# A four-layer graph network: slots for near edges alone in layer 0, a ranking of nodes for each layer, paced scatters and bulk loads

## The chip, the cores and the metric

The kernel runs on one core of a Trainium2 chip. The metric is the device time of one execution in microseconds (us), so lower is better. The core's engines are PE (matrix multiply; its weight loads are listed as PEld), DVE (vector), ACT (scalar, activation functions), POOL (general purpose) and SP (here only an issuer of DMAs). Each engine works through its own instructions strictly in order, so an instruction that waits holds up everything queued behind it on that engine. That holds for the DMAs that SP and POOL issue too.

## The reference

There are 128 graphs of 64 nodes with 128 features, `x[128,64,128]`, and one weighted adjacency `adj[128,64,64]` for all layers. Four layers follow each other, each as `x = layernorm(x + layer(x, adj))`. Layers 0 and 1 are convolutions with a filter that a small network makes from each edge's length; they are the costly ones.

```
layer 0:  f  = exp(coeff * (d - offset)^2)                 # 20 values per pair of nodes
          W  = ssp(f @ fw1 + fb1) @ fw2 + fb2              # 128 values per pair of nodes
          W *= 0.5 * (cos(d * pi / 5) + 1) * (d < 5)       # nothing is left from the cutoff 5 on
          agg[i] = sum_j y[j] * W[i,j],   y = x @ w_in2f
layer 1:  the same shape with 64 Gaussians; W *= adj twice, so only nonzero entries count
layers 2, 3: two graph convolutions with a normalised adjacency
```

In layer 0 an entry `adj = 0` is a distance of zero and not a missing edge: it has the full weight, and one and the same filter. Entries of 5 and more add nothing in layer 0, but they do count in layer 1. Counted from the reference's own inputs, a node has 15.88 nonzero entries on average, 13.22 of them below the cutoff.

## The kernel before, in words

Only nonzero entries go through the filter network. A first stage counts the nonzero entries of each node, ranks the 64 nodes of a graph by that count, and gives rank class `r` (eight nodes each) a fixed number of slots, `CAPS[r]`. Eight classes have 34+23+...+15 = 165 slots together, a graph has 8 x 165 = 1320 (`GSLOTS`). If some graph does not fit, a flag sends the whole job to `dense_stack` afterwards; this does not happen with these inputs.

Graphs are handled in 64 pairs (`NP`), and eight pairs form a set. For each set, `compact`

- scatters the adjacency rows into rank order in DRAM, with 8 indirect DMAs from POOL (one per pair, `perm`, line 807), and reads them back (`ad`, line 815);
- takes the largest entries of each row eight at a time on DVE: `max` (line 823), `max_index` (826), `match_replace` (830). `ROUNDS` says how often per class, 24 rounds in all;
- copies the values into `dc` (POOL, line 837) and the indices into `jc` (ACT), makes the cutoff weight `rc` with seven DVE instructions and one sine on ACT, and `a2` (the squares, for layer 1) on POOL, and stores all four to DRAM (lines 851, 852, 877, 878).

Set 0 is compacted ahead of the main loop. The other seven are interleaved with the first twenty pairs or so of it, by a queue called `early`, from which up to ten steps are taken per chunk.

The main loop takes layer 0's 64 pairs and then layer 1's. A pair is done in three chunks of 440 slots per graph. For a pair, `loads` brings `d`, `j` and the weight `w` from DRAM, each copied to many partitions (lines 907 to 918; buffers for two pairs). Per chunk there are:

- ACT: the Gaussians of the next pair (`gaussians`, the square and the exponential of `d`);
- DVE: `hot`, a weighted one-hot matrix that selects a neighbour for each slot (line 1276);
- PE: `px` (first filter layer, line 1291), `pw` (second, line 1304), `pg` (gathering the neighbours' features with `hot`, line 1316);
- ACT: `h` twice (softplus as exponential and logarithm) and `g` (a copy out of PSUM);
- DVE: `m = (pw + b2) * g` (line 1329), and after a pair's last chunk eight `agg` sums over slots (line 1345).

The chunks are software-pipelined: `message` works on the chunk from three iterations back, `filter_out` and `gather` on the one from two back. After four pairs (a quad) `node_after` does the output network, `zero_share` (the share of zero entries, read from `perm`), the way back from rank order (from `code_dram`), and a layernorm, whose power of -0.5 runs on POOL (line 1064). Layers 2 and 3 (`graph_convs`) run beside layer 1 for quads that are done.

The order on each engine is made at build time by the framework's scheduler from the order of the calls, its own estimates and the dependencies; it may hoist work. A DRAM tile is tracked as a whole: two scatters into one `perm` tile are ordered, and the second waits until the first has landed. Before the change the scheduler placed the scatters of sets 0 to 4 in turn (set 0, 1, 2, 3, 4, 0, 1, ...), so set 0's eighth scatter is the 36th of the program.

Of the kernel before, what the change touches and what calls it, by code (L numbers as in the profile page):

```python
# [11 lines left out]
F32 = mybir.dt.float32  # L12
# [6 lines left out]
P = 128  # L19
A = 64  # L20
# [18 lines left out]
CAPS = (34, 23, 21, 20, 19, 17, 16, 15)  # L39
ROUNDS = tuple(-(-k // 8) for k in CAPS)  # L40
BASES = tuple(sum(CAPS[:r]) for r in range(8))
SLOTS = sum(CAPS)
GSLOTS = 8 * SLOTS
CHUNK = GSLOTS // 3
# [530 lines left out]
def sparse_stack(ctx: ExitStack, tc: tile.TileContext, t: dict, out: bass.AP, flag):  # L575
# [26 lines left out]
    place = const.tile([NB, A], F32, name="place")  # L602
    odd = const.tile([P, 4 + NS], F32, name="odd")
    nc.gpsimd.memset(odd, 0.0)
    with (
# [4 lines left out]
        some = pre.tile([NB, A, A], BF16, name="some")  # L610
        for q in range(4):
            cut = slice(16 * q, 16 * (q + 1))
            nc.sync.dma_start(entries[:, cut, :], adj[:, cut, :])
            nc.vector.tensor_scalar(some[:, cut, :], entries[:, cut, :], 0.0, None, ALU.is_gt)

        def count(v, name):
# [11 lines left out]
        degree = count(some, "degree")  # L628


        tie = pre.tile([NB, A], I32, name="tie")
        nc.gpsimd.iota(tie, pattern=[[-1, A]], base=A - 1, channel_multiplier=0)
        key = pre.tile([NB, A], F32, name="key")
        nc.vector.tensor_copy(key, tie)
        nc.vector.scalar_tensor_tensor(key, degree, float(A), key, ALU.mult, ALU.add)
        before = pre.tile([NB, A, A], BF16, name="before")
        nc.vector.tensor_tensor(
            before, key.unsqueeze(1).to_broadcast([NB, A, A]),
            key.unsqueeze(2).to_broadcast([NB, A, A]), ALU.is_gt,
        )  # L640
        rank = count(before, "rank")

        r_i = pre.tile([NB, A], I32, name="r_i")
        nc.vector.tensor_copy(r_i, rank)
        p_i = pre.tile([NB, A], I32, name="p_i")
        nc.vector.tensor_scalar(p_i, r_i, 7, 3, ALU.bitwise_and, ALU.logical_shift_left)
        nc.vector.tensor_scalar(r_i, r_i, 3, None, ALU.logical_shift_right)
        nc.vector.tensor_tensor(p_i, p_i, r_i, ALU.bitwise_or)
        nc.vector.tensor_copy(place, p_i)


        caps = pre.tile([NB, 8], F32, name="caps")
        most = pre.tile([NB, 8], F32, name="most")
        for r in range(8):
            nc.gpsimd.memset(caps[:, r : r + 1], float(CAPS[r]))
            nc.gpsimd.memset(most[:, r : r + 1], 8.0 * r)
        over = pre.tile([NB, 8, A], F32, name="over")
        nc.vector.tensor_tensor(
            over, degree.unsqueeze(1).to_broadcast([NB, 8, A]),
            caps.unsqueeze(2).to_broadcast([NB, 8, A]), ALU.is_gt,  # L660
        )
        number = pre.tile([NB, 8], F32, name="number")
        nc.vector.tensor_reduce(number, over, AX.X, ALU.add)
        nc.vector.tensor_tensor(number, number, most, ALU.is_gt)
        nc.vector.tensor_reduce(odd[:, 0:1], number, AX.X, ALU.add)

        below = pre.tile([NB, A * A], F32, name="below")
        nc.scalar.activation(
            below, entries.rearrange("g i j -> g (i j)"), AF.Relu, scale=-1.0, accum_out=odd[:, 1:2]
# [3 lines left out]
        for i, (w, b, k) in enumerate(  # L673
# [13 lines left out]
            nc.vector.tensor_scalar(odd[:, 2 + i : 3 + i], b1, X_LIMIT, None, ALU.is_gt)  # L687
# [42 lines left out]
    row_i = const.tile([P, 3], I32, name="row_i")  # L730
    nc.gpsimd.iota(row_i, pattern=[[0, 3]], base=0, channel_multiplier=1)
    nc.vector.tensor_scalar(row_i[:, 1:2], row_i[:, 1:2], 15, 6, ALU.bitwise_and, ALU.logical_shift_left)
    nc.vector.tensor_scalar(row_i[:, 2:3], row_i[:, 2:3], 1, 6, ALU.bitwise_and, ALU.logical_shift_left)

    row = const.tile([P, 3], F32, name="row")
    nc.vector.tensor_copy(row, row_i)

    near_i = const.tile([P, 1], I32, name="near_i")
    nc.vector.tensor_scalar(near_i, row_i[:, 0:1], 63, None, ALU.bitwise_and)
    near = const.tile([P, 1], F32, name="near")  # L740
    nc.vector.tensor_copy(near, near_i)
# [3 lines left out]
    nc.vector.tensor_scalar(goes, place, row[:, 1:2], None, ALU.add)  # L745
    tp = ps_n.tile([P, 512], F32, tag="n", name="goes_t")
    nc.tensor.transpose(tp[0:A, 0:P], goes, ident)
    index = const.tile([P, NP], U32, name="index")
    by_pair = tp[0:A, 0:P].rearrange("i (p b) -> i p b", b=2)
    for b in range(2):  # L750
        nc.vector.tensor_copy(index[b * A : (b + 1) * A, :], by_pair[:, :, b])

    code = const.tile([P, A], BF16, name="code")
    nc.vector.tensor_scalar(code, place, row[:, 2:3], None, ALU.add)
    code_dram = dram.tile([NB, A], BF16, name="code_dram")
    nc.sync.dma_start(code_dram, code)

    a_all = const.tile([P, NP, A], F32, name="a_all")
    a_pairs = adj.rearrange("(p b) i j -> (b i) p j", b=2)
    x_all = const.tile([P, NP, C], F32, name="x_all")  # L760
    x_pairs = x.rearrange("(p b) n c -> (b n) p c", b=2)
    perm = [dram.tile([16 * A, A], F32, name=f"perm{s}") for s in range(NS)]
    slots = {
        name: [dram.tile([P, SLOTS], dt, name=f"{name}_dram{s}") for s in range(NS)]
        for name, dt in (("d", F32), ("j", BF16), ("rc", F32), ("a2", F32))
# [30 lines left out]
    def compact(sets):  # L796
# [5 lines left out]
        n = len(sets)  # L802
        dc = cpt.tile([P, n * SLOTS], F32, tag="dc", name=f"dc{sets[0]}")
        jc = cpt.tile([P, n * SLOTS], BF16, tag="jc", name=f"jc{sets[0]}")
        for i, s in enumerate(sets):
            for p in range(8 * s, 8 * (s + 1)):
                nc.gpsimd.indirect_dma_start(  # L807
                    out=perm[s][:, :],
                    out_offset=bass.IndirectOffsetOnAxis(ap=index[:, p : p + 1], axis=0),
                    in_=a_all[:, p, :],  # L810
                    in_offset=None,
                )
                yield
            ad = cpt.tile([P, 8, A], F32, tag="ad", name=f"ad{s}", bufs=2)
            nc.sync.dma_start(ad, perm[s].rearrange("(q r) j -> q r j", r=8))
            yield
            top = cpt.tile([P, 8, 40], F32, tag="top", name=f"top{s}", bufs=2)
            at = cpt.tile([P, 8, 40], U16, tag="at", name=f"at{s}", bufs=2)
            for k in range(max(ROUNDS)):
                now = [r for r in range(8) if ROUNDS[r] > k]  # L820
                cut = slice(8 * k, 8 * (k + 1))
                for r in now:
                    nc.vector.max(out=top[:, r, cut], in_=ad[:, r, :])
                    yield
                for r in now:
                    nc.vector.max_index(out=at[:, r, cut], in_max=top[:, r, cut], in_values=ad[:, r, :])  # L826
                    yield
# [617 lines left out]
```

## Time and profile before

| | us |
|---|---|
| median of 3 runs | 2127.33 |
| lowest, highest | 2122.57, 2143.56 |
| the profiled execution, whole | 2122.68 |
| its span in the profile | 2120.9 |
| first `px` matmul of pair 0 | 117.8 |
| first `hot` of layer 0, first `hot` of layer 1 | 122.0, 998.7 |
| busy: PE, DVE, ACT, POOL | 1775.3, 1692.6, 1489.6, 210.1 |

Span and whole execution differ by 1.8 us. The profile's times start with the first instruction. Where a stretch table is shown, its columns are: the stretch in us, its length, the busy time of PE, PEld, DVE, ACT and POOL with the number of instructions in brackets, the granted clock of PE as a share of full speed, the mean busy share of the 16 DMA engines, and GB/s. In a list in order of time, a line gives start and duration, engine, source line, operation and tiles, and in brackets the idle time of the engine before it with what ended that.

### The profile page before, as it was taken

What the parts mean: (1) busy time and instruction counts of PE and PEld (TensorE: products, weight loads), DVE (VectorE), ACT (ScalarE), POOL (GpSimd) and SP (SyncE); (2) the same over time, 40 slices, a digit from 0 to 9 for tenths busy, and PEclk for the clock granted to TensorE, in tenths of its full rate; (3) what the DMA queues carried; (4) which work ended last, traced back from release to release, by engine and by line L of the source; (5) the groups of instructions that cost most, each with busy time, mean ns of one, the idle gap of its engine ahead of it and who ended that gap; (6) DMA issues with size and microseconds to landing.
All of it is one profiled execution on the core that took longest, in us unless ns stands there. A gap on an engine that the chain in (4) does not pass through costs nothing.

```text
span 2120.9 us, 22583 instructions
## 1 busy us (share of the span) xinstructions
PE 1775.3 (84%) x6827; PEld 794.1 (37%) x6827; DVE 1692.6 (80%) x4476; ACT 1489.6 (70%) x1662; POOL 210.1 (10%) x296
## 2 busy tenths in 40 slices
PE   0087888899999999999988988888888898888874
PEld 0032333333333333333344444444444444444433
DVE  3395999988888888888778887887888888878863
ACT  0075778798888888888877766776677776777730
POOL 4714000000000000000000010010000101001010
PEclk9987989999999999999999999999999999999985
DMA  7154443444444444445544444534345344453300
GB/s 198 41 130 105 102 100 88 107 111 108 108 108 108 117 114 116 113 113 123 133 122 96 120 104 99 130 91 120 92 111 125 95 121 104 102 133 89 94 5 7
DMA packets 111392, 222.77 MB, mean 105 GB/s; under 512 B 35972, under 2 KB 61596, under 8 KB 111260
## 3 DMA queue, kind: packets, MB, share of 16 engines
q1 hardware_dynamic: 105040, 218.06, 41.9%
q0 software_dynamic: 2048, 2.10, 0.3%
q10 hardware_dynamic: 4172, 1.07, 0.3%
q8 instruction: 56, 0.92, 0.2%
q14 instruction: 76, 0.62, 0.1%
HBM read 212.49 MB, written 8.67 MB: 104 GB/s over the span
## 4 chain that ended last, share of the span: by engine, by line
PE 35%; DVE 32%; ACT 16%; issue 6%; DMA 5%; POOL 5%; SPq 0%; ACTq 0%; DVEq 0%; POOLq 0%
PE pw L1304 11%; DVE m L1329 7%; DVE agg L1345 7%; PE pg L1316 7%; PE px L1291 6%; ACT h L713 5%; ACT g L713 4%; DVE hot L1276 4%; ACT d L713 3%; DVE x_all L1067 2%; ACT na L713 2%; DMA d<-d_dram 2%; PE hw L1213 2%; POOL perm L807 2%; POOL rs L1064 2%
## 5 line engine op out<-in xcount | busy, mean ns | idle before, releaser
L713 ACT ACTIVATE g<-pg 128x880 f32<-128x880 f32 x384 | 344.4, 897 | 306.8 <-PE pg L1316 247.7
L1316 PE MATMUL pg<-hot,ys 64*128 64x440 f32 x1536 | 420.0, 599 | 37.2 <-ACT g L713 37.1
L1345 DVE TENSOR_REDUCE agg<-m 128x16 f32<-128x544 f32 (+7 forms) x1024 | 442.6, 487 | 0.0
L1304 PE MATMUL pw<-h,w_L_gnn_fw 128*128 128x440 f32 x768 | 354.9, 573 | 56.0 <-DVE m L1329 52.3
L713 ACT ACTIVATE h<-h,half 128x880 f32<-128x880 f32 (+1 forms) x385 | 394.6, 1025 | 8.3
L1304 PE MATMUL pw<-h,w_L_gnn_W2T 128*128 128x440 f32 x768 | 333.8, 557 | 3.1 <-DVE m L1329 3.1
L1329 DVE SCALAR_TENSOR_TENSOR m<-pw,c_L_gnn_fb,g 128x440 f32<-128x440 f32 x384 | 240.4, 667 | 62.7 <-ACT g L713 62.5
L1329 DVE SCALAR_TENSOR_TENSOR m<-pw,c_L_gnn_b,g 128x440 f32<-128x440 f32 x384 | 242.5, 667 | 57.5 <-ACT g L713 56.5
L1276 DVE SCALAR_TENSOR_TENSOR hot<-j,near,w 128x440 f32<-128x440 bf16 x384 | 249.9, 672 | 21.7 <-PE pg L1316 21.5
L713 ACT ACTIVATE h<-px,c_L_gnn_b 128x880 f32<-128x880 f32 x192 | 189.9, 989 | 77.2 <-PE px L1291 77.2
L1316 PEld LDWEIGHTS pg<-hot,ys 64*128 64x128 f32 x1536 | 124.3, 189 | 277.3 <-ACT h L713 86.1
L1064 POOL TENSOR_TENSOR rs<-rs,neg_half 128x4 f32<-128x4 f32 x64 | 64.5, 1008 | 1514.3 <-DVE rs L1063 1502.3
L1304 PEld LDWEIGHTS pw<-h,w_L_gnn_fw 128*128 128x128 f32 x768 | 130.4, 196 | 215.0 <-DVE m L1329 122.2
L1291 PE MATMUL px<-d,w1t 64*128 64x440 f32 x768 | 197.6, 563 | 4.4 <-ACT h L713 4.4
L1291 PE MATMUL px<-d,fw 32*128 32x440 f32 x768 | 198.8, 594 | 2.5 <-ACT d L713 1.5
L713 ACT ACTIVATE h<-px,c_L_gnn_fb 128x880 f32<-128x880 f32 x192 | 190.2, 991 | 8.8 <-PE px L1291 2.7
L1304 PEld LDWEIGHTS pw<-h,w_L_gnn_W2T 128*128 128x128 f32 x768 | 133.5, 194 | 150.3 <-issue 70.3
L713 ACT ACTIVATE d<-d,neg_off 96x880 f32<-96x880 f32 (+1 forms) x128 | 154.0, 1203 | 15.2 <-DMA d<-d_dram 14.2
L1291 PEld LDWEIGHTS px<-d,fw 32*128 32x128 f32 x768 | 59.1, 187 | 130.0 <-ACT h L713 64.8
L1291 PEld LDWEIGHTS px<-d,w1t 64*128 64x128 f32 x768 | 73.3, 190 | 71.2 <-issue 39.9
L713 ACT ACTIVATE jc<-at 128x16 bf16<-128x16 uint16 (+7 forms) x64 | 11.3, 215 | 109.4 <-DVE at L826 106.8
L713 ACT ACTIVATE d<-d 128x1320 f32<-128x1320 f32 x64 | 83.1, 1299 | 0.5
(182 smaller groups left out, 1754.6 us busy)
## 6 DMA issues: line engine op xcount, KB each, us to landing
j<-j_dram SPq DMA_DIRECT2D x256, 165.0 KB
w<-rc_dram SPq DMA_DIRECT2D x128, 330.0 KB
w<-a_dram SPq DMA_DIRECT2D x128, 330.0 KB
d<-d_dram SPq DMA_DIRECT2D x128, 330.0 KB
d<-d_dram SPq DMA_DIRECT2D x192, 110.0 KB
x_all<-in_x_dram SPq DMA_DIRECT2D x8, 512.0 KB
cb<-code_dram SPq DMA_DIRECT2D x32, 128.0 KB
out_dram<-gz SPq DMA_DIRECT2D x16, 256.0 KB
```

The lines of the kernel that those rows point to most:

```text
L713: last = nc.scalar.activation(out_, in_, func, **kw)
L807: nc.gpsimd.indirect_dma_start(out=perm[s][:, :], out_offset=bass.IndirectOffsetOnAxis(ap=index[:, p : p + 1], axis=0), in_=a_all[:, p, :] ...
L1064: nc.gpsimd.tensor_tensor(rstd, rstd, neg_half[:, 0:n], ALU.pow)
L1067: nc.vector.tensor_scalar(dst[:, s, :], y[:, s, :], mv[:, s, 0:1], rstd[:, s : s + 1], ALU.subtract, ALU.mult,)
L1213: nc.tensor.matmul(ps[:, s, :], lhsT=lhs(s), rhs=rhs(s), start=True, stop=True)
L1276: nc.vector.scalar_tensor_tensor(hots[n][:, at], j[:, at], near, wt[:, at], ALU.is_equal, ALU.mult)
L1291: nc.tensor.matmul(ps[:, b, 0:CHUNK], lhsT=w["w1"][rows, :], rhs=d[rows, col : col + CHUNK], start=True, stop=True,)
L1304: nc.tensor.matmul(ps[:, 0:CHUNK], lhsT=c["w"]["w2"], rhs=c["h"][:, b, :], start=True, stop=True)
L1316: nc.tensor.matmul(ps[:, b, 0:CHUNK], lhsT=y[rows, :], rhs=hots[c["n"]][rows, at], start=True, stop=True,)
L1329: nc.vector.scalar_tensor_tensor(messages[n][:, b, at], c["pw"][b][:, 0:CHUNK], c["w"]["b2"], c["g"][:, b, :], ALU.add, ALU.mult,)
L1345: nc.vector.tensor_reduce(av[:, :, r], v[:, :, BASES[r] : BASES[r] + CAPS[r]], AX.X, ALU.add)
```

## The change

The counting stage now also counts the entries below the cutoff, and ranks the nodes twice: `places[0]` by the number of nonzero entries below the cutoff, `places[1]` by the number of all nonzero entries. Each layer gets its own slots: layer 0 has 141 per class set (chunks of 376 slots), layer 1 has 162 (chunks of 432).

`compact` works in the order of `places[0]`. It turns the values around (zero becomes -1e30, the rest their negatives), so `max` now finds the nearest edges first. It takes 30 rounds instead of 24, because all edges of a row are kept for layer 1, up to 40. The first ones become layer 0's slots (`pack(0, s)`). A new step `spread(s)` scatters the sorted rows once more, into the order of `places[1]`, with 8 more indirect DMAs (`rows1`), reads them back and packs layer 1's slots (`pack(1, s)`). For set 0 it first repeats the 8 scatters of the adjacency with the extra column that carries the second rank (`perm_again`).

The bulk loads of `a_all` and `x_all` for sets 1 to 7 no longer stand ahead of the loop: `load_set(s+1)` is issued in the loop, after the loads of a pair. The scatters are held back by `mark(n)`, a one-column copy on POOL that reads pair `n`'s `hot`: a set's first scatters come after `hot` of its pair 1 (modulo 8), the second ones after that of pair 4. The cosine weight is made per set, with one sine for each of eight sets (before: five sines for all). Layer 1's weights and the constants of layers 2 and 3 are asked for later. `early` gives up to 8 steps per chunk instead of 10.

```diff
-CAPS = (34, 23, 21, 20, 19, 17, 16, 15)
+CAPS = ((30, 21, 18, 17, 16, 14, 13, 12), (33, 23, 21, 19, 18, 17, 16, 15))
+ROUNDS = (5, 4, 4, 4, 4, 3, 3, 3)
...
+            nc.vector.tensor_scalar(near[:, cut, :], entries[:, cut, :], CUTOFF, None, ALU.is_lt)
...
+        rank(0, close)
+        rank(1, degree)
+        crowded(0, close)
+        crowded(1, degree)
...
+    def mark(n):
+        return nc.gpsimd.tensor_copy(marks[:, n % 2 : n % 2 + 1], hots[n][:, 0:1])
+
+    def scatter(into, rows, at, behind):
+        with tc.issue_after(behind.ins) if behind is not None else nullcontext():
+            nc.gpsimd.indirect_dma_start(
+                out=into, out_offset=bass.IndirectOffsetOnAxis(ap=at, axis=0),
+                in_=rows, in_offset=None,
+            )
...
+    def compact(s, behind=None):
+        ad = cpt.tile([P, 8, A + 1], F32, tag="ad", name=f"ad{s}", bufs=2)
+        for p in range(8 * s, 8 * (s + 1)):
+            scatter(perm[s][:, :], a_all[:, p, 0 : A + (s > 0)], index[:, p : p + 1], behind)
+            yield
+        nc.sync.dma_start(ad[:, :, 0 : A + (s > 0)], perm[s].rearrange("(q r) j -> q r j", r=8))
...
+        nc.vector.tensor_scalar(zero, av, 0.0, FAR, ALU.is_equal, ALU.mult)
+        nc.vector.tensor_tensor(av, zero, av, ALU.subtract)
...
+        yield from pack(0, s, top, at)
+        tops[s] = ad, comb, at
+
+    def spread(s, behind):
+        ad, comb, at = tops.pop(s)
+        if s == 0:
+            for p in range(8):
+                scatter(perm_again[:, :], a_all[:, p, :], index[:, p : p + 1], behind)
+                yield
...
+        goes = cpt.tile([P, 8], U32, tag="goes", name=f"goes1_{s}")
+        nc.vector.tensor_scalar(goes, ad[:, :, A], row[:, 4:5], None, ALU.add)
+        nc.gpsimd.tensor_copy(comb[:, :, 1, :], at)
+        yield
+        for r in range(8):
+            scatter(
+                rows1[s].rearrange("q a k -> q (a k)"),
+                comb[:, r, :, :].rearrange("p a k -> p (a k)"), goes[:, r : r + 1], behind,
+            )
+            yield
+        rows = cpt.tile([P, 8, 2, 40], F32, tag="rows", name=f"rows_{s}")
+        nc.sync.dma_start(rows, rows1[s].rearrange("(q r) a k -> q r a k", r=8))
+        yield
+        yield from pack(1, s, rows[:, :, 0, :], rows[:, :, 1, :])
...
-    for s in range(1, NS):
-        nc.sync.dma_start(a_all[:, part(s), :], a_pairs[:, part(s), :])
-        nc.sync.dma_start(x_all[:, part(s), :], x_pairs[:, part(s), :])
...
+            if k == 0 and n < NP:
+                if n % 8 == 0 and n + 8 < NP:
+                    load_set(n // 8 + 1, slot_data[n + 1][3])
+                if n % 8 == 1 and n + 8 < NP:
+                    early.append(compact(n // 8 + 1, mark(n)))
+                if n % 8 == 4:
+                    early.append(spread(n // 8, mark(n)))
+                if n == NP // 2:
+                    layers.append(filter_layer(1))
+                if n == NP - 3:
+                    early.extend((settle(), late_constants()))
...
-        run(early, 10)
+        run(early, 8)
```

## The prediction

> **What bounds the kernel now.** I read the page first (busy shares, the strip of slices), then the table of stretches, then the list in order of time.
>
> ```profile
> PE 1775.3 (84%) x6827; PEld 794.1 (37%) x6827; DVE 1692.6 (80%) x4476; ACT 1489.6 (70%) x1662; POOL 210.1 (10%) x296
> ...
> PE   0087888899999999999988988888888898888874
> ...
> DVE  3395999988888888888778887887888888878863
> ```
>
> No single engine is full; the strips show three parts. In the first two slices (53 us each) PE does nothing: the head, until the first `hot` at 122.0. In slices 4 to 7 DVE reads 9 and PE 8. Then PE reads 9.
>
> ```profile
> 220.00:320.00 100.00, 82.72 (x289) 33.31 (x288) 96.31 (x423) 71.76 (x96) 6.20 (x24) 0.91 0.42 106
> 527.41:629.97 102.56, 97.99 (x374) 39.39 (x372) 84.24 (x184) 87.79 (x96) 2.02 (x2) 1.00 0.45 110
> ```
>
> While sets are compacted, DVE is busy 96% and sets the pace; afterwards, 51.2 us per four pairs, PE is busy 96% and DVE has 18% left. Layer 0 lasts from 122.0 to 998.7, 876.7 us. What an edit costs thus depends on whether it falls on a stretch with DVE work to spare.
>
> **Fewer slots.** PE has 12.25 us per pair (97.99 / 8). Per chunk the chain gives `pw` 1.67, `pg` 0.94, `px` 0.94, together 3.55; times 376/440 that is 3.03, so a pair of layer 0 needs 10.7. DVE has 10.53 per pair. The sums of 544 and 240 elements take 711 and 394 ns, 1.04 ns per element; 64 elements less in 6 `m` and 3 `hot` save 0.60 and 384 less in `agg` 0.40, leaving 9.5. Layer 1 goes from 440 to 432: about 70% of its 1046 us follows the slots, so 1.8% x 0.85 of that saves **12 us**.
>
> **Compaction.** Eight `MAX8` take 1.10 us, an index search 0.195, a replacement 0.19. 24, 24 and 16 of them cost 11.0 us per set; 30, 30 and 22 cost 14.1. Some fifteen other DVE rows of 0.1 to 0.6 us (turning values, ties, mask, weight) bring 4.2, the degrees 1.3: 19.6 per set. Before, this fell in the first 300 us; now it lies in layer 0 up to pair 55, beside DVE work. DVE then has 9.5 + 19.6/8 = 11.95 per pair, 95.6 per set, 99.5 at 96% busy. It, not PE, sets the pace there. Three pairs of each set have no ranking work in the built order and go by PE: 10.7 at a granted clock of 0.95 (between the 0.91 and 1.00 of the two stretches) is 11.2, against DVE's 10.1 with what is left of the set, so 3.5 more. That makes 103 us per set without any new wait, against 102.5 in the steady part before.
>
> **The scatters become a chain.** This is the change's largest unknown.
>
> ```profile
> 106.93 0.97 POOL L807 DMA_INDIRECT perm<-a_all,index  x1 [0.30 <-issue]
> 109.30 1.07 POOL L807 DMA_INDIRECT perm<-a_all,index  x1 [1.40 <-DMA perm<-a_all,index]
> ...
> 117.17 0.99 POOL L807 DMA_INDIRECT perm<-a_all,index  x1 [1.40 <-DMA perm<-a_all,index]
> ```
>
> Before, scatters of five (later three) sets took turns, 1.27 us apart, so that each had long landed when the next into the same tile came. In the built program of the new kernel a set's eight stand one behind the other, and each waits for the one before. What a landing takes, two rows tell. The scatter at 109.30 waited for the one issued at 104.27, 5.0 us earlier, with a pair's loads in the queues; the one at 117.17 for that of 111.95, 5.2. In the quiet,
>
> ```profile
> 72.17 0.96 POOL L807 DMA_INDIRECT perm<-a_all,index  x1 [0.30 <-issue]
> ...
> 74.33 0.32 SPq L815 DMA_DIRECT2D ad<-perm  x1
> ```
>
> set 0's eighth had landed 2.2 us after its issue. So a step of the chain (issue, landing, next issue) costs 2.3 to 5.2 us. The loop's DMA share is 0.45, and 2.3 + 0.45 x 2.8 gives **3.5**, my value.
>
> What waits for the chain: in DVE's order, the turning of values (line 889) stands 17.7 us of work behind the `hot` that releases the chain, 19 us at the pace above. The chain needs 0.6 + 8 x 3.5 + 0.4, and the read-back 3.5 (in the old loop 3.0 to 5.0), so 32.5: DVE stands still for **13.5 us**, and all of `hot`, `m`, `agg` queue behind it. The second chain has six scatters ahead of the copies into `dc` on POOL, which DVE's line 853 needs 15.6 us after the mark: 0.6 + 5 x 3.5 + 2.6 = 20.7, **5 us** more. Because DVE sets the pace there, nothing covers these stalls: `pw` can't run ahead further than its PSUM buffers, which `m` frees.
>
> Behind the waiting instructions stand other things. On SP the read-backs of both chains have the `d` loads of a pair two ahead behind them. `d` is wanted by ACT two chunks after DVE goes on, some 8 us, and such a load lands in about 6, so I add nothing; without that cover it would be up to 6 per set. On POOL the layernorm's power of every second quad stands behind the second chain, its read-back and eight copies, 42 us after the mark; its user on DVE comes after 41.5 us of work plus the 5 us stall, so it is hidden too, and is 3 late at steps of 5. POOL's own new work, 16 scatters, a mark, and some 20 copies of 0.2 us per set, is some 22 us of 120. 18.6 per set, seven sets: **130 us**. At steps of 2.3 us it is 4 per set, at 5.2 it is 41.
>
> [...]
>
> The scatter's own time on POOL is 0.97 us on average with DVE idle (45 to 74 us) and 0.97 beside `MAX8` and its kin (94 to 104), so I add nothing for DVE. [...] No copy of DVE lies beside a scatter in those rows, while the new scatters lie in the loop. [...]
>
> **The rest of layer 0.** Each set has its own sine; the two table loads of 1.28 on ACT are a bubble. ACT is near 10.7 per pair too; 0 to 20, I take 10. The two powers of 10.6 us on POOL, on the chain before at 165, move behind set 7's scatters and ahead of a layernorm's: 6. In sum: pairs 0 to 7 at PE's pace (8 x 10.7 at a clock of 0.93) 92, six sets 6 x 103 = 618, pairs 56 to 63 without compaction 8 x 11.0 = 88, stalls 130, 10 and 6: 944, **67 more** than 876.7.
>
> **The head.** Before `index`, the second count adds 3.8 us, the second comparison 4.4 and its count 3.1, small ones 3: the first scatter comes 14.3 us later, at 41.7. But set 0's eighth is now the eighth and not the 36th: eight steps of 2.4 end at 61, against 74.3. The read-back took 5.1 to the first `MAX8` (79.47), so rounds start near 67 and take 14. From the old rounds' end (101.2) to the first `hot` were 21 us, so `hot` comes near 103, 19 earlier. The old rounds contain 11 us (82 to 93) in which DVE waited for nothing that the profile shows; whether that returns is open, and scatter steps of 5 would take 21. Range 25 gained to 5 lost; I take **15 gained**. That the bulk loads (6 MB) leave the head is inside this: in the loop they add to a DMA share of 0.45 and cost at most what the step's upper bound holds.
>
> **The sum**, against the profiled execution: 2122.7 + 67 - 15 - 12 = **2163 us**, 1.7% above the median of 2127.33. 1% is about what a measurement can tell from no change.
>
> **Rivals.**
> - *The chain is short* (the other side, faster). Scatters land in the gaps between the loads, at 2.3 per step, and lines 889 and 853 find their data nearly there. Per set the stalls are 8 x step - 14.5 and 5 x step - 12.4, so it decides below 2.9 us per step: there they are 11 in all, and the total is 1% under the median. For it: 2.2 in the quiet, and a stall of DVE itself empties the queues. Against: the waits of 5.0 and 5.2. At 2.3: 130 falls to 28, 2163 - 102 = about 2060, with the full gain of the head 2050.
> - *The chain is loaded throughout*, because the bulk loads go into the loop just ahead of the first scatters: 5 us per step, 38 per set, 2163 + 136 = 2300. For it: the same two rows. Against: half of the time the DMA engines are idle.
> - *The slots do not suffice*, and the dense version runs as well. Counted from the reference's inputs, no graph exceeds the new classes; I give it nothing.
>
> **How the numbers follow.** Steps between 3 and 4 us, 2110 to 2215: 0.45, of which 0.17 is within 1%. Short chain: 0.32, faster. Loaded chain: 0.18. Other causes 0.05, split. So faster 0.34, the same 0.17, slower 0.49. The range takes in nearly all of the short chain and most of the loaded one: 2040 to 2280.
>
> **What would show it.** In the new profile: `px` and `pw` near 0.49 and 0.48 us each instead of 0.58 and 0.55; DVE idle before line 889, released by the read-back, about 13 us seven times; POOL's scatters 3.5 us apart with the DMA of the one before as releaser; the first `hot` near 105; layer 1 beginning near 1050. I am wrong if line 889 does not wait, if PE rather than DVE is full in pairs 8 to 55, or if DVE, PE and ACT, all at 10.7 to 12 us per pair, hold each other up more than 96% busy allows.

## The result, and the profile after

The changed kernel takes **2197.87 us** (median of 4 runs, 2184.42 to 2204.98) against 2134.48 us of the kernel before (median of 4, one of them measured beside the changed kernel). The ratio is 1.029, with a 95% interval of 1.021 to 1.038: slower by about 3%. The forecast was 2163, with a range of 2040 to 2280. Runs more than 1.5% above their kernel's fastest (one of experiment 1, two of experiment 5) are left out of the ratios below, but not out of the medians.

The profiled execution took 2202.33 us (span 2200.5), 79.7 more than the one of before. It splits as follows; "head" is the time to the first `hot` of layer 0, "layer 1" what follows the first `hot` of layer 1.

| | before | after | difference | forecast |
|---|---|---|---|---|
| head | 122.0 | 97.6 | -24.4 | -15 |
| layer 0 | 876.7 | 961.2 | +84.5 | +67 |
| layer 1 and the end | 1122.2 | 1141.7 | +19.5 | -12 |

From the page of the changed kernel, busy times and three strips (forty slices of 55 us, in tenths):

```profile
PE 1793.1 (81%) x6828; PEld 850.8 (39%) x6828; DVE 1679.1 (76%) x4824; ACT 1404.3 (64%) x1727; POOL 305.4 (14%) x482
...
PE   0378898887978886898989888898888998888874
...
DVE  5577787778787775886888887788878877778773
...
PEclk9978888898988887898999999999999999999985
```

DVE, which the prediction held to be full in layer 0, reads 7 and 8 there. PE has fewer slots to work through and yet is busy 18 us longer than before. The strip of the granted clock points to why: 8 through most of layer 0, where the kernel before has 9 from its seventh slice to the end of layer 0:

```profile
PEclk9987989999999999999999999999999999999985
```

The stretch table of the changed kernel; the columns are those explained with the profile of before (the number in tenths or hundredths behind POOL is the granted clock). The rows are pairs 16 to 23, 56 to 63, and, in layer 1, 32 to 39:

```profile
328.00:450.70 122.70, 102.21 (x374) 46.77 (x372) 95.94 (x337) 82.46 (x116) 22.77 (x40) 0.85 0.41 100
...
953.60:1058.80 105.20, 93.93 (x380) 42.97 (x379) 77.04 (x185) 80.17 (x106) 12.04 (x20) 0.92 0.42 105
...
1565.80:1702.50 136.70, 121.96 (x482) 59.61 (x480) 109.23 (x257) 92.33 (x101) 11.62 (x14) 0.93 0.43 104
```

The row of before for the same eight pairs of layer 1:

```profile
1506.30:1636.50 130.20, 115.56 (x482) 56.61 (x480) 110.24 (x257) 93.59 (x101) 11.45 (x14) 0.99 0.46 109
```

In layer 0 a set takes 123 us, though DVE has only 96 us of work. In layer 1 a set has 2% fewer columns than before and DVE and ACT are busy 1 us less, and yet it takes 6.5 us longer: PE is busy 6.4 us longer, at a clock of 0.93 instead of 0.99.

What ends the pauses in layer 0 is seen in the list in order of time. First POOL and DVE in the third set:

```profile
340.37 1.08 POOL L832 DMA_INDIRECT perm<-a_all,index  x1 [0.17 <-issue]
343.30 0.95 POOL L832 DMA_INDIRECT perm<-a_all,index  x1 [1.85 <-DMA perm<-a_all,index]
348.05 0.96 POOL L832 DMA_INDIRECT perm<-a_all,index  x1 [3.80 <-DMA perm<-a_all,index]
...
363.27 0.96 POOL L832 DMA_INDIRECT perm<-a_all,index  x1 [1.50 <-DMA perm<-a_all,index]
```

```profile
365.69 0.69 DVE L1100 TENSOR_TENSOR a_all<-a_all,eye 128x512 f32<-128x512 f32 x1 [9.43 <-DMA perm<-a_all,index]
...
368.71 0.42 DVE L889 TENSOR_SCALAR zero<-ad 128x512 f32<-128x512 f32 x1
```

The eight scatters stand one behind the other, 3.3 us apart, each released by the one before. DVE stands still for 9.4 us until the last has landed. The instruction that waits is line 1100: it adds the identity into `a_all` for the degrees, and so may not start while a scatter still reads `a_all`. The scheduler has put it ahead of line 889, which needs the read-back.

Later in the same set, ACT:

```profile
410.74 1.28 ACT L733 ACT_TABLE_LOAD   x1
418.38 0.41 ACT L733 ACTIVATE w<-w,half_pi 128x141 f32<-128x141 f32 x1 [6.36 <-DVE w L857]
418.81 1.28 ACT L730 ACT_TABLE_LOAD   x1
```

The sine waits 6.4 us for DVE, which had waited 3.5 us at line 853 for the copies into `dc`; these stood on POOL at 414.80, behind six scatters of the second chain. All `h` and `g` queue behind the sine; the next of them begins at 420.11. Over the five sets from 206.9 to 820.7 the sine waits for DVE for (us in total, times, longest)

```profile
ACT w L733 <- DVE w L857: 31.7, 5, 8.1
```

The waits of DVE from pair 8 to 55, as groups:

```profile
DVE a_all L1100 <- DMA perm<-a_all,index: 54.7, 6, 10.3
DVE m L1404 <- ACT g L733: 39.9, 31, 3.8
DVE w L853 <- POOL dc L846: 18.3, 6, 4.4
...
DVE dinv L1110 <- POOL dinv L1109: 9.7, 1, 9.7
```

### The profile page after: what moved, and what is told of

Read it like the earlier page. It is cut to its first block, busy times and chain, and to the rows that moved or that the text cites. A ratio compares the mean times of both kernels' runs of the same rounds, so it can differ in the third digit from the quotient of the medians.

```text
span 2200.5 us, 23302 instructions
## 1 busy us (share of the span) xinstructions
PE 1793.1 (81%) x6828; PEld 850.8 (39%) x6828; DVE 1679.1 (76%) x4824; ACT 1404.3 (64%) x1727; POOL 305.4 (14%) x482
## 4 chain that ended last, share of the span: by engine, by line
PE 21%; DVE 12%; ACT 12%; issue 4%; DMA 3%; POOL 1%; SPq 0%; DVEq 0%; POOLq 0%; ACTq 0%
PE pw L1376 6%; ACT g L733 4%; ACT h L733 3%; PE pg L1389 3%; ACT d L733 3%; DVE m L1404 3%; PE px L1363 2%; DVE agg L1420 2%; PE hw L1284 2%; DVE x_all L1138 2%; PE o L1293 2%; PE o L1291 2%; DMA cb<-code_dram 1%; POOL rs L1135 1%; DVE hot L1348 1%
## 5 line engine op out<-in xcount | busy, mean ns | idle before, releaser
L733 ACT ACTIVATE g<-pg 128x752 f32<-128x752 f32 (+1 forms) x384 | 321.0, 836 | 388.7 <-PE pg L1389 255.2
L1389 PE MATMUL pg<-hot,ys 64*128 64x376 f32 (+1 forms) x1536 | 432.0, 596 | 38.8 <-ACT g L733 38.6
L1420 DVE TENSOR_REDUCE agg<-m 128x16 f32<-128x336 f32 (+11 forms) x1024 | 418.6, 460 | 0.3
L1376 PE MATMUL pw<-h,w_L_gnn_fw 128*128 128x376 f32 x768 | 331.9, 550 | 87.4 <-DVE m L1404 87.4
L733 ACT ACTIVATE h<-h,half 128x752 f32<-128x752 f32 (+2 forms) x385 | 371.8, 966 | 8.1
L1376 PE MATMUL pw<-h,w_L_gnn_W2T 128*128 128x432 f32 x768 | 342.4, 570 | 3.0 <-DVE m L1404 2.8
L1404 DVE SCALAR_TENSOR_TENSOR m<-pw,c_L_gnn_b,g 128x432 f32<-128x432 f32 x384 | 239.6, 660 | 56.5 <-ACT g L733 55.6
L1404 DVE SCALAR_TENSOR_TENSOR m<-pw,c_L_gnn_fb,g 128x376 f32<-128x376 f32 x384 | 215.9, 600 | 75.5 <-ACT g L733 75.1
L1348 DVE SCALAR_TENSOR_TENSOR hot<-j,row,w 128x376 f32<-128x376 bf16 (+1 forms) x384 | 235.6, 633 | 21.7 <-PE pg L1389 20.4
L1363 PE MATMUL px<-d,w1t 64*128 64x432 f32 x768 | 201.3, 575 | 4.6 <-ACT h L733 4.6
```

Source lines behind the costliest of these rows:

```text
L733: last = nc.scalar.activation(out_, in_, func, **kw)
L1348: nc.vector.scalar_tensor_tensor(hots[n][:, at], j[:, at], near, wt[:, at], ALU.is_equal, ALU.mult)
L1363: nc.tensor.matmul(ps[:, b, 0:n], lhsT=w["w1"][rows, :], rhs=d[rows, col : col + n], start=True, stop=True,)
L1376: nc.tensor.matmul(ps[:, 0 : c["size"]], lhsT=c["w"]["w2"], rhs=c["h"][:, b, :], start=True, stop=True)
L1389: nc.tensor.matmul(ps[:, b, 0:n], lhsT=y[rows, :], rhs=hots[c["n"]][rows, at], start=True, stop=True,)
L1404: nc.vector.scalar_tensor_tensor(messages[n][:, b, at], c["pw"][b][:, 0:size], c["w"]["b2"], c["g"][:, b, :], ALU.add, ALU.mult,)
```

## The experiments

Each kernel was timed against the kernel before on the same chip, whose medians there lay between 2131 and 2136 us. "Set" is eight pairs. "Half clock" is the time for which the trace's clock records grant PE half its speed.

**1. Eight tensors in place of one chain.**

```
-    perm = [dram.tile([16 * A, A + (s > 0)], F32, ...) for s in range(NS)]
+    perm = [dram.tile([P, A + (p > 7)], F32, ...) for p in range(NP)]
...
-            scatter(perm[s][:, :], a_all[:, p, ...], ...)
+            scatter(perm[p][:, :], a_all[:, p, ...], ...)
```

> The eight scatters of a set go into eight DRAM tensors and are read back by eight transfers; the second chain (for layer 1) stays. Theory A, a stall costs its length and then as much again, because PE, left without work, is granted half its clock afterwards: the wait of 9.4 us of DVE (now attributed to line 1100, the degrees) goes in seven sets, and with it 4 to 7 us of half clock; a set takes 108 to 111 us instead of 123, and the whole 85 to 105 us less than the changed kernel's 2198: about 2100. Theory B, a stall costs its length alone: 66 less, 2132, the granted clock of layer 0 stays at 0.85. Theory C, DVE's work (96 us per set) and the coupling of the engines set the 123, the wait merely lies in their slack: under 25 less, above 2170.

Measured: 2177.33 us, ratio 1.026 (1.017 to 1.034). POOL now issues a set's eight scatters without waiting for landings (1.27 us apart in the trace of experiment 5, which keeps this edit), and the head falls by 13 us (first `hot` at 84.8). But four of the sets from the third on still take 117 to 123 us. Theory C seemed to hold; the reason shows in experiment 3.

**2. The copies on DVE.**

```
-            nc.gpsimd.tensor_copy(dc[:, to], d[:, r, 0 : CAPS[layer][r]])
+            (nc.gpsimd if layer else nc.vector).tensor_copy(dc[:, to], ...)
```

> The eight small copies into dc (line 846, layer 0 only) go from POOL, where they stand behind five scatters of the second chain, to DVE; the two chains stay. Theory A: the wait of line 853 (4.4 us per set) goes, the wait of ACT's sine for line 857 (6.4 to 7.2 us) falls to 3 or less, and PE's half clock behind it gets shorter; 5 to 9 us per set, minus 1 us for the copies: 30 to 60 us less than 2198. Theory B (length alone): 3 us per set, about 20 less. Theory C: ACT's wait is set by where line 853 to 857 stand among the m and hot of DVE's order, and nothing changes: within 10.

Measured: 2196.41 us, ratio 1.032 (1.026 to 1.038): nothing. The wait at line 853 is gone and the sine's wait falls from 31.7 us in five sets to 18.8. (In the set shown above the copies stood behind six scatters, not five.) But `goes` (line 937), which DVE has later in its order, now waits 15.2 us for the second chain's scatters, about what line 853 waited before.

**3. Both.**

> Eight tensors and the copies on DVE. Theory A: both savings add, a set takes 101 to 106 us at a granted clock of 0.93 or more, 2040 to 2075 in all, and the kernel beats the one before the change. Theory B: 2100 to 2115. Theory C: above 2160.

Measured: 2171.74 us, ratio 1.019 (1.014 to 1.025). That fits theory C by the number, but the waits of DVE in five sets show that the stall had moved rather than gone:

```profile
DVE m L1409 <- ACT g L733: 40.7, 26, 3.9
DVE a_all L1107 <- DMA d<-d_dram: 35.3, 5, 7.3
DVE goes L944 <- DMA rows<-comb,goes: 20.5, 5, 6.1
```

With shorter chains the scheduler placed the degrees earlier in DVE's order, ahead of the `hot` of the set's third pair instead of behind it. They still overwrite what the scatters read, and they waited 7 us. (The profile names a load of `d` as what came last. That it was the scatters is inferred: in experiment 1 two of the five waits at this line are put down to them, and in the fourth set here the wait ends 3.0 us after the last scatter's issue.) So experiments 1 to 3 did not test what they were meant to test.

**4. Layer 1 with the old slots.**

```
-CAPS = ((30, 21, 18, 17, 16, 14, 13, 12), (33, 23, 21, 19, 18, 17, 16, 15))
+CAPS = ((30, 21, 18, 17, 16, 14, 13, 12), (34, 23, 21, 20, 19, 17, 16, 15))
```

> The slots of layer 1 alone go back to the classes of before (165 per eight nodes instead of 162, 440 columns per chunk instead of 432); to make room, the tile zt shares its buffer with em. Layer 0 stays as it is (961 us from its first hot to that of layer 1). Theory A, the shorter chunks of layer 1 leave PE idle just long enough at each quad's end that its clock halves (0.93 against 0.99 before): with longer chunks the clock returns, a set of layer 1 takes 130 to 132 us instead of 136.6, and the whole 20 to 35 us less, though there is more work. Rival, the time of layer 1 follows its slots: 1.8% more, 8 to 14 us longer. Rival, the lower clock belongs to that execution and not to the kernel: the clock of layer 1 differs between executions of both kernels, and the times are within 10.

Measured: 2185.12 us, ratio 1.027 (1.022 to 1.033). The times alone do not tell it clearly from the changed kernel. The profile does: sets of layer 1 take 130.5 to 133.2 us with more slots against 130.4 to 136.7 with fewer. The table under experiment 9 gathers all runs.

**5. All the waits that were found taken away.** On top of experiment 3 (a set's eight scatters are also given out in one step):

```
+            with tc.issue_after(last_hot[0].ins):       # the degrees, behind layer 0
                 nc.vector.tensor_add(part_, part_, eye...)
...
+            for _ in range(12): yield                   # then the sine
             act(w, w, AF.Sin, bias=half_pi, scale=-PI)
...
         nc.sync.dma_start(rows, rows1[s]...)
+        for _ in range(16): yield                       # then layer 1's packing
```

> e3_both and four moves more: the degrees (lines 1100 and 1101, which in e3_both came earlier in DVE's order and waited up to 7.3 us for the same scatters) are kept behind the last hot of layer 0; the sine is issued one and a half chunks later than its argument; layer 1's packing one and a half chunks after its read-back; a set's scatters go out together. By the trace of e3_both that takes 7 us (degrees), 4 us (goes, line 937 of the changed kernel), and 4 to 5 us (ACT's sine) of waits out of each set of 120. Theory A, the waits and the half clock behind them make the difference: a set takes 101 to 108 us at a granted clock of 0.95 or more, in all 2050 to 2090, faster than the kernel before the change. Theory C, the engines hold each other up as long as DVE has 96 us of work per set, in whatever order: 114 to 120 us per set, 2130 to 2170.

Measured: 2115.9 us (10 runs), ratio 0.989 (0.985 to 0.993): the sign turns, by 1%. Two of its sets in the stretch table:

```profile
310.00:417.10 107.10, 97.89 (x374) 44.20 (x372) 94.85 (x343) 82.30 (x116) 23.12 (x32) 0.92 0.46 115
417.10:524.90 107.80, 96.94 (x374) 44.94 (x374) 94.78 (x342) 82.37 (x116) 22.34 (x32) 0.94 0.47 113
```

These two take 107 to 108 us with 95 us of DVE work (96 in the changed kernel), 15 us less than there. That is about the sum of two waits that went (8.9 of line 1100 per set, 6.3 of the sine); which of the four moves brought how much was not measured. The total lies between the ranges of theories A and C. The sets from the third to the seventh, 105 to 111 us, speak against C's 114 to 120, but they have a clock of 0.91 to 0.95 where A expected 0.95 or more. Two sets remain long, the second with 121.5 and the last with 118.5, since ACT's `jc` copies wait 13.4 and 9.2 us there for the second chain's read-back, and since in the last one DVE has all the degrees to do and waits 10.5 us for their powers.

**6. The degrees alone moved.** The first edit of experiment 5, nothing else.

> The changed kernel with the degrees alone kept behind the last hot of layer 0; chains and copies stay. If line 1100 only stood in front of line 889 in the queue, line 889 inherits the wait for the read-back, 7 to 13 us per set, and the time stays within 15 us of 2198. If the degrees made DVE wait for nothing that the turning of values needs so early, the stall of 9.4 us goes: 60 to 100 us less.

Measured: 2196.09 us, ratio 1.029 (1.025 to 1.033): no change. Line 889 inherits the wait:

```profile
DVE zero L889 <- DMA ad<-perm: 49.9, 5, 11.4
```

10 us per set, where the prediction had 13.5 for this line.

**7. The slots alone, in the kernel before.**

```
-CAPS = (34, 23, 21, 20, 19, 17, 16, 15)
+CAPS = (30, 21, 18, 17, 16, 14, 13, 12)
```

> The kernel before the change, with the slots alone: the classes of layer 0 of the changed kernel (141 per eight nodes, 376 columns per chunk) in both layers, everything else, the number of rounds too, as before. Edges beyond a class are left out, above all in layer 1; the test that would start the dense version compares with the old classes. Theory A, the slots are worth what PE's rows say, where PE has no holes: from 589 us on a set of eight pairs of layer 0 takes 86 to 92 us instead of 102.4, at a granted clock of 1.00; layer 1's sets 114 to 120 instead of 130; 1930 to 1980 in all. Rival, the gain is eaten by the clock, because a PE with less work has holes after which it gets half its clock: layer 0 from 589 us on 95 to 101 per set, granted clock 0.93 or less, more than 2030 in all.

Measured: 1984.3 us, ratio 0.932 (0.928 to 0.936). A set of layer 0 from the fourth on:

```profile
543.20:633.20 90.00, 88.16 (x374) 40.19 (x372) 76.69 (x183) 77.62 (x97) 2.01 (x2) 1.00 0.43 110
```

90.0 us against 102.4 at the same full clock. The slots are worth what PE's rows said, 12.4 us per set, where PE runs at full clock. In layer 1 the same cut brings only 4 us per set: 126.1 us at a clock of 0.96, where 114 to 120 were expected. The total lies 4 us above the expected range.

**8. One stall of known length, in the kernel before.**

```
+            seen = nc.gpsimd.tensor_copy(mark, hots[n - 1][:, 2 * CHUNK : 2 * CHUNK + 1])
+            with tc.issue_after(seen.ins):
+                nc.gpsimd.tensor_tensor(power, power, neg_half[:, 0:60], ALU.pow)   # and 24 more
+            held = nc.vector.tensor_copy(power[:, 0:1], power[:, 1:2])   # ahead of hot
```

> The kernel before the change, with one stall of DVE put into each of the last four sets of layer 0, which run at 102.4 us and a granted clock of 1.00: in pairs 35, 43, 51 and 59 a small copy of DVE, ahead of hot, waits for two powers on POOL that begin after the hot of the pair before; 14 us of POOL against 4.8 us of DVE work in between, so a wait of about 9. Theory A: a set takes 9 us and 5 to 8 us of half clock more, 116 to 120, in all 55 to 70 us more. Theory B: 9 us more, 35 to 40 in all, no lower clock but in the stall. Theory C: slack swallows it, under 15 in all.

Measured: 2167.61 us, ratio 1.018 (1.014 to 1.022), about 36 us more. DVE's wait and a set that has it:

```profile
DVE power L1284 <- POOL power L1283: 37.4, 4, 9.3
```

```profile
700.40:813.10 112.70, 101.91 (x374) 41.36 (x373) 84.63 (x185) 88.01 (x97) 16.23 (x5) 0.94 0.41 101
```

Four waits of 9.3 us make the first of the sets 8.6 us longer and the other three 10.3. PE is granted half its clock for some 10 us per set more, and in the three its busy time grows by 4 us, but most of that seems to fall into the slack that the engines have. Theory B holds for the time: a stall of this kind costs about its length. It does not hold for the clock. In the set shown the wait ends at 741.4, and half clock lasts from 738.0 to 751.6.

**9. The hole of PE in layer 1 filled with work that is thrown away.**

```
             filter_out(started)
+            if started["n"] >= NP + GS and started["s"] == 2 and started["k"] == 1:
+                again(filtered, 2)      # the last gather's products, twice more, into the same tile
```

In the changed kernel, once per quad of layer 1, PE stands idle behind a `pw` until DVE's `m` frees a PSUM buffer:

```profile
1619.79 1.72 PE L1376 MATMUL pw<-h,w_L_gnn_W2T 128*128 128x432 f32 x4
1624.27 1.09 PE L1274 MATMUL nT<-ident,blk 128*128 128x128 f32 x4 [2.77 <-DVE m L1404]
```

The kernel before has the same hole, of the same length:

```profile
1560.71 1.74 PE L1304 MATMUL pw<-h,w_L_gnn_W2T 128*128 128x440 f32 x4
1565.23 0.63 PE L1203 MATMUL nT<-ident,blk 128*128 128x128 f32 x4 [2.78 <-DVE m L1329]
```

The layer has twelve such holes between its second and last eight pairs, all of 2.8 us. A hole counts as hit here when half clock begins before its end or within 0.5 us of it: before, 4 of the 12 are hit, in the changed kernel 10 (within 1.8 us: 6 and 12). In the two shown, the four transposes `nT` take 1.09 us after the change and 0.63 before. The stretch table of the changed kernel around the hole, and that of the kernel before (the third number from the right is the granted clock):

```profile
1621.00:1625.00 4.00, 1.23 (x6) 0.72 (x4) 4.00 (x11) 3.61 (x3) 0.00 (x0) 0.86 0.00 0
1625.00:1629.00 4.00, 4.00 (x14) 1.73 (x12) 2.33 (x6) 0.89 (x1) 1.55 (x2) 0.50 0.38 92
```

```profile
1562.00:1566.00 4.00, 1.22 (x8) 0.63 (x8) 4.00 (x10) 3.59 (x3) 0.06 (x1) 1.00 0.00 0
1566.00:1570.00 4.00, 4.00 (x17) 1.84 (x16) 3.39 (x7) 2.50 (x3) 1.43 (x2) 1.00 0.38 100
```

> The changed kernel, with two gathers of layer 1 (pg, four matrix products of 432 columns) done a second time in each quad, just where PE stands idle for 2.8 us behind the second pw of the quad's third pair; the result is the same, PE has 1.9 us more work per quad, some 28 us in all. Theory A, the hole of 2.8 us is what takes the clock down to half for 6.8 us in nearly every quad of the changed kernel (97 us at half clock between the second and the last eight pairs of layer 1, against 41 in the kernel before): with a hole of 0.9 us the clock stays, a set of eight pairs takes 129 to 131 us instead of 136.6, and the whole is 25 to 40 us faster in spite of the extra work. Rival: the work is simply added, 0 to 28 us slower.

Measured: 2158.22 us, ratio 1.011 (1.006 to 1.015): 40 us faster than the changed kernel, with more work for PE and the same result. The hole is 1.1 us now, and the transposes are fast again:

```profile
1606.72 1.72 PE L1405 MATMUL pg<-hot,ys 64*128 64x432 f32 x8
1609.57 0.63 PE L1274 MATMUL nT<-ident,blk 128*128 128x128 f32 x4 [1.13 <-DVE m L1417]
```

The six sets from the second of layer 1 on, in all profiled executions (half clock: between 104 and 911 us after the layer's first `hot`):

| layer 1 | executions | six sets, us | half clock, us |
|---|---|---|---|
| 440 columns | before, 4, 8 | 791 to 795 | 41 to 48 |
| 432 columns | changed, 1, 2, 3, 5, 6, 11 | 803 to 815 | 79 to 104 |
| 432, hole filled | 9, 10, 12 | 775 to 776 | 20 to 27 |
| 376 columns | 7 | 755 | 65 |

The ranges do not overlap. With the hole filled (1.1 to 1.2 us left) none is hit in experiments 9, 10 and 12, by either count. So the eight columns less made layer 1 slower because PE's clock was halved more often. Experiment 4 also gave the tile `zt` another buffer; experiment 9 leaves columns and buffers as they are.

**10. All repairs together.** Experiment 5 with layer 1's packing 40 instead of 16 steps behind its read-back, `goes` in two buffers, the degrees and their powers a set at a time in the loop, and the filled hole of experiment 9:

```
+                if n % 8 == 6 and n > 8:
+                    degrees(n // 8 - 1)      # lines 1100 to 1113 for eight pairs, powers too
```

> e5_no_waits with what its trace still shows waiting taken away: layer 1's packing five chunks behind its read-back instead of two (ACT waited 13.4 us in the second set and 9.2 in the last), the tile goes twice (DVE waited 10.6), the degrees and their powers eight pairs at a time, a set behind, instead of all ahead of layer 1 (10.5 us of wait for the powers, 10 us of work in the last set), and the repeated gathers of e9_refill_hole. By theory A the second set falls from 121 to about 108, the last from 118 to about 100, layer 1 by 25 to 35: 2116 less 55 to 70, that is 2045 to 2065, 3% to 4% faster than the kernel before. Theory C: other waits take their place, above 2095.

Measured: 2069.77 us (6 runs), ratio **0.973** (0.969 to 0.977). It beats both kernels, though it misses the 2045 to 2065 of theory A. The last set of layer 0 fell to 101.2, and the six sets of layer 1 by 40 us, more than expected. The second set did not fall (123.8: ACT's `jc` still waits 13.7 us for the second chain's read-back there, and 8.0 in the last set too). The third to the seventh take 108 to 116, on average 4 us more than in experiment 5, with 19.8 us at half clock per set instead of 15.0; why is open:

```profile
424.30:533.00 108.70, 97.22 (x374) 44.97 (x373) 96.39 (x348) 82.80 (x116) 25.77 (x34) 0.94 0.46 112
```

Part of the lead over the kernel before comes from filling the hole, which that kernel could be given too; this was not tried.

**11. The bulk loads ahead of the loop.**

```
-    load_set(0)
+    for s in range(NS):
+        load_set(s)
```

> The changed kernel with the bulk loads of all eight sets issued ahead of the loop again, right behind set 0's; nothing else is moved. If the pacing of the loads is what shortened the head, the first hot comes 10 to 25 us later than 97.6 and the whole is 5 to 25 us slower. If the loads in the loop make the scatters slow, their steps fall to 2.5 us, the wait at line 1100 nearly goes, and the whole is 30 us or more faster. If neither, within 10.

Measured: 2198.51 us, ratio 1.032 (1.028 to 1.037): no difference. The first `hot` comes at 96.7, and the scatters of the chains that rank layer 0 are 3.0 to 3.4 us apart as before. Pacing the loads neither helps nor hurts.

**12. Fewer rounds.** Experiment 10 with 21 rounds of the search instead of 30, at the same places:

```
-ROUNDS = (5, 4, 4, 4, 4, 3, 3, 3)
+ROUNDS = (4, 3, 3, 3, 2, 2, 2, 2)
```

> e10_all_repairs with 21 rounds of MAX8, index search and replacement per set instead of 30 (13 replacements instead of 22), at the same places of the order; edges of nodes with more neighbours than the rounds hold are left out, above all in layer 1, and the test for full rows is off. By the rows of the profile that takes 9 x 0.14 + 9 x 0.20 + 9 x 0.19 = 4.8 us of DVE's 96 us out of a set. If DVE's work sets the pace of the sets that rank, as the prediction said, a set falls by 4.5 to 5.5 us, in all 30 to 40 less than 2070. If the holes of PE and the clock set it (e10: 108 to 116 us per set at a clock of 0.88 to 0.94 with DVE busy 87%), a set falls by 2 or less, in all under 15.

Measured: 2019.09 us, ratio 0.946 (0.941 to 0.951), 51 us less than experiment 10. Sets three to seven take 103.7 us on average instead of 111.3, with DVE busy 91.7 instead of 96.3:

```profile
304.20:407.20 103.00, 92.70 (x374) 42.85 (x374) 91.59 (x302) 83.86 (x117) 25.86 (x34) 0.95 0.48 119
```

4.6 us of DVE work taken out bring 7.6 us, above both ranges. That speaks for the prediction's view that DVE's work sets the pace of these sets, and against the rival of 2 us or less, though DVE is busy 88% there, not 96%. The 3 us beyond DVE's own share go along with less half clock in these sets, 15.0 us per set instead of 19.8.

## Why the prediction came out as it did

**Direction and mechanism held.** Serial scatters do hold up DVE in each set, and this turns a gain into a loss: without the waits the kernel is 1% faster than before (experiment 5), with them 3% slower. How clear the loss is, is in part luck: 49 us of it come from two terms that the prediction had wrong (the last eight pairs and layer 1, below). Without them the profiled execution would have taken some 2154 us, 1.5% more than the one of before. The rival "the chain is short" needed steps under 2.9 us. The chains that rank layer 0 ran at 3.1 to 3.6 per step in the loop, mean 3.3, against 3.5 taken and 2.3 to 5.2 as bounds; no step of any chain was under 2.4. DVE's work hardly made scatters slower on POOL: all 136 took 0.95 to 1.22 us, mean 0.98, and the eleven that had a copy of DVE beside them 1.03 on average, against 0.97 for the others.

**The set of 122 us was right as a sum, with two parts that were off against each other.** The prediction had 103 us without waits and 18.6 of waits. Experiments 5 and 10 show sets of 105 to 116 (the third to the seventh) without these waits, and the changed kernel's are 15 us longer than those of experiment 5. That the sum came out is thus in part luck. The step "99.5 at 96% busy" failed: that row of 96% came from sets with 126 us of DVE work in 131, in which, presumably, everything else could wait for DVE. With 95 us of DVE work beside 82 on ACT and about 88 on PE at full clock (experiment 7), DVE reaches 83 to 91%. As "I am wrong if" had it, the engines hold each other up more. That the time follows DVE's work is confirmed in direction by experiment 12. Six sets were forecast at some 744 us with the sines and powers, and took 746.7.

**The place of the waits.** Line 889 waits only once in the loop, 9.3 us in the first of the seven chains. In the other six line 1100 waits in front of it, 8.1 to 10.3 us, for the landing of the scatters rather than for the read-back behind them. By the letter that is the prediction's own sign "I am wrong if line 889 does not wait", though the chain is the cause all the same; with the degrees out of the way line 889 waits as predicted, 10 us rather than 13.5 (experiment 6). The second wait was taken as 5 us of DVE at line 853. It is 2.7 to 4.4 there, and it shows on ACT, whose sine stops 6.3 us per set. The prediction priced the sines as a bubble of 10 us for two table loads and did not ask what the sine itself would wait for.

**The last eight pairs failed: 88 forecast, 105.2 measured.** "Pairs 56 to 63 without compaction 8 x 11.0" was right for six of them (953.6 to 1019.2, 10.9 each). The seventh took 25.7, where the same slots without a chain took 11.8 (experiment 7). ACT's copies into `jc` for layer 1 wait for the read-back of the last second chain:

```profile
ACT jc L733 <- DMA rows<-rows: 8.9, 1, 8.9
```

The prediction followed the second chain to `dc` on POOL and to the layernorm's power, but not to `jc` on ACT, which stands in the queue of `h` and `g`. The eight pairs are 17 us of the 39 by which the forecast fell short. The wait itself is 9 of them, and PE has half its clock from 1023.2 to 1040.2 behind it. That the wait causes all of the seventh pair's 14 us is argued: no experiment took it away. In experiment 10 it is still 8.0 us, and the pair takes 22.1.

**Layer 1 failed with its sign: 12 faster forecast, 19.5 slower measured.** The step was "1.8% x 0.85 of that", of the 70% of 1046 us that follow the slots (which makes 11 rather than 12). It took for granted that time follows slots at an unchanged clock. The clock of these sets fell from 0.99 to 0.93. Experiment 9 shows the cause by filling the hole: 35 us less in the six sets of the profile. This is 31.5 us of the shortfall.

**The head** gained 24.4 rather than 15, near the end of 25 that the prediction gave for it. The first scatter came at 39.0 instead of 41.7. Pacing the loads has no part in it (experiment 11).

**The slots** were sized rightly in time: 12.25 to 10.7 us of PE per pair forecast, 102.4 to 90.0 per set measured, 1.55 per pair both times (experiment 7). That is in part luck. PE's busy time fell by only 1.2 per pair (97.8 to 88.2 per set), and the rest came out of its idle time. The prediction scaled `px` and `pw` with their columns, by 0.85, to 0.49 and 0.48 us. At full clock they take 0.526 and 0.497 in experiment 7, against 0.580 and 0.553 before, only 0.91 and 0.90 of it. In the changed kernel they take 0.578 and 0.550 on average over layer 0, against 0.594 and 0.573 before; there about 287 us of layer 0 run at half clock against 76 before.

What stays open: how much of the 105 to 116 us of a set without the two waits is due to the half clock itself (167 and 157 us of it remain in layer 0 in experiments 5 and 10), and how each of the four moves of experiment 5 counts alone.

## What to carry to other kernels

When a serial chain is moved into a loop, list every engine queue that holds a consumer of it, the late ones too (here `jc` and the sine on ACT), and price each: a 9.3 us stop cost 8.6 to 10.3 us per set. An experiment that shortens a wait has to be read by its list of waits before its time is believed, since a scheduler that reorders can move the wait elsewhere. And a smaller matrix load is only worth its share while the clock of the matrix engine holds: with a hole of 2.8 us once per quad, 2% fewer columns were 1% to 3% slower, and useless products in the hole were worth 40 us.

## What was not expected of the hardware

The granted clock of PE has two values in these traces, full and half, and its half-speed intervals mostly (50 of 53 in the changed kernel's trace) have lengths of 3.4, 6.8, 10.2, 13.7 and 17.1 us, multiples of 3.41. In each of the 14 traces all falls of the clock (53 in the changed kernel's) lie on one grid of 3.413 us, to within 2 ns. Holes of 2.8 us, shorter than a step of this grid, were followed by half clock in 4 of 12 cases before the change, in 4 of 12 and 3 of 12 in experiments 4 and 8 with the same 440 columns, and in 10 of 12 after it. Even the holes of 1.95 us that the 376 columns of experiment 7 leave are followed by it, in 4 of 12 cases within 0.5 us and in 11 of 12 within 1.8; holes of 1.1 to 1.2 us (experiments 9, 10 and 12) never are. Why a hole is followed by half clock, the traces do not show.

Which quads, seems to depend on how the hole lies against this grid. In the changed kernel two such holes end at 1624.27 and 1692.62, 68.35 us apart, 20.0 times 3.413, and with them begins a row of seven holes that are all hit, 68.2 to 68.4 us apart; half clock begins 0.37 to 0.56 us before the end of each. Whole sets come out near multiples too: 136.6 us is 40.0 steps of the grid and 133.1 (experiment 4) 39.0, while the sets of before that were not hit, with 130.2, are 38.1. The sets of experiment 7, with 126.1, are 36.9 and do not fit as well. In the row of seven each quad takes 20 steps, so that the next hole meets the grid at the same place. That this locking is what keeps the clock down is an inference from these numbers; that the hole does it is shown by experiment 9 (20 to 27 us at half clock in its table with the hole filled, 79 to 104 without). How long a hole must be, or how it must lie against the grid, does not come out of these traces.
